# B laid out in DRAM and SBUF with four states side by side per time step, and its product with x walked in that layout by GpSimd

## The chip, the cores and the metric

One core of a Trainium2 chip runs the whole program. The metric is the device time of one execution in microseconds (us). The engines of the core run their own queues of instructions in order and wait for each other through semaphores: PE (TensorE, matmuls; PEld is its loading of weights), DVE (VectorE), ACT (ScalarE), POOL (GpSimd), and SP (SyncE), which issues the DMAs here.

## What is computed

The input x has 32 sequences (batches) of 512 steps with 256 channels. Three layers follow each other, each added to its own input: a feed-forward layer with blockwise 4-bit quantization (counted half), a selective state-space layer, and the first layer once more. The change lies in the state-space layer, whose input is normalized first:

```python
BC = x @ W_in + b_in
Bm, Cm = (BC[..., :N], BC[..., N:])            # N = 16 states
dt = jax.nn.softplus((x @ W_dt1 + b_dt1) @ W_dt2 + b_dt2)
dt = jnp.clip(dt, 1e-07, 1000000.0)
tmp = A * dt[..., None]
A_bar = jnp.exp(tmp)
B_barX = jnp.expm1(tmp) / tmp * dt[..., None] * Bm[:, :, None, :] * x[..., None]
...
_, h = jax.lax.associative_scan(combine, (A_bar, B_barX), axis=1)   # h[t] = A_bar[t] h[t-1] + B_barX[t]
return jnp.sum(h * Cm[:, :, None, :], axis=-1) + D * x
```

So for each channel and each of 16 states there is one recurrence over 512 steps. Bm and Cm depend on the step and the state, not on the channel.

## The kernel before

All data are 32-bit floats apart from the quantizer's bf16 helpers. The loop runs over the 32 batches. For each batch there are an input load, `ffn` (first layer), `ssm` (the state-space layer), `ffn` again and an output store; several batches are in flight at once.

In `ssm`, channels lie on the 128 partitions, in NC = 2 halves (index c), and the 512 steps lie along the free dimension. L is 512, N is 16, NG = 2 states make a group and XG = 4 states make a bigger one. Per batch:

- `project` (PE) and `project bias` (ACT, L1658) make `bc`, a tile of 96 partitions: 64 rows that lead to dt, 16 rows of B and 16 of C, one state per partition, 512 steps each.
- `rows` (SP, L1661) stores the 32 rows of B and C in DRAM, one row of 2 KB per state. This is done since B and C are needed on all 128 partitions.
- `load b` (SP, L1697) reads four states at a time back, the same 8 KB for all 128 partitions, into `bn`; `load c` (SP, L1707) reads two states at a time, 4 KB for each partition, into `cn`. Two buffers exist of each.
- `x b` (POOL, L1701) multiplies `bn` with x, in two halves of 256 steps, into `bx`. x does not depend on the state, so it is repeated over the four states. `bn` and `bx` hold state after state, 512 steps (2 KB) each, but the instruction goes through them step by step with the four states innermost. Each instruction has 256 x 4 = 1024 elements per partition. Two buffers of `bx` exist.
- For each state, `exp` (ACT, L1714) and `tanh` (ACT, L1717) make A_bar and a half-way value of expm1, and three DVE instructions of 512 elements follow: `e` (L1722) finishes expm1 in PSUM (tile `eb`), `e x b` (L1725) multiplies it with 1/A and with this state's `bx`, and `scan` (L1728) runs the recurrence into `hs`. `e x b` reads `eb` from PSUM and `bx` from SBUF and writes `eb`.
- `h c` (POOL, L1731) multiplies two states of `hs` with `cn`, 1024 elements per partition without gaps; `sum states` (PE, L1737) adds the states up in PSUM.

POOL also does part of the feed-forward layer: `product` (L1611) and the quantizer's `value` (L1482; tiles x_q and h_q), where a block's scale is repeated over its 16 elements. DVE makes the quantizer's `quotient` (L1457), the tops of the blocks (L1451) and the statistics of the norms (L1414, L1416).

The order of the work is written out. Every operation is given to a planner (class `Plan`) with a name, and tables (`WHEN` for the batches in the middle, four others for the first two and last two) hold a due time for each name and count; `PERIOD` = 3379 is added per batch. `Plan.run` puts out operations by due time among those whose inputs have been put out, so the tables set the order on each engine's queue, SP's among them. Nothing is reordered after that: an instruction that waits holds up all that stand behind it on its engine. On SP, each batch's `rows` is followed by loads of the old batch's C and by the new batch's first loads.

Of the kernel before, what the change touches and what calls it, by code (L numbers as in the profile page):

```python
# [31 lines left out]
    "in load": (307,),  # L32
    "ffn 0 stats": (1353, 1162, 433, 1372),
    "ffn 0 mean": (1534, 1207, 2280, 3568),
    "ffn 0 var + eps": (-3072,),
    "ffn 0 rstd": (3743,),
    "ffn 0 - mean": (4137,),
    "ffn 0 shift": (4475,),
    "ffn 0 normal": (4908, 2828, 6516, 4907),
    "ffn 0 x top": (6592,),  # L40
    "ffn 0 x scale": (6720,),
    "ffn 0 x rinv": (6812,),
    "ffn 0 x quotient": (6837,),
    "ffn 0 x square": (6261,),
    "ffn 0 x curve": (6856,),
    "ffn 0 x grid": (4711,),
    "ffn 0 x rounded": (6976,),
    "ffn 0 x value": (6142,),
    "ffn 0 xqT turn": (4710, 4914),
    "ffn 0 xqT turned": (7146, 7155),  # L50
    "ffn 0 tile 0 gate": (7210, 7319),
    "ffn 0 tile 0 silu": (7161, 2717),
    "ffn 0 tile 0 up": (7401, 7534),
    "ffn 0 tile 0 up copy": (7351, 6546),
    "ffn 0 tile 0 product": (7515,),
    "ffn 0 tile 0 h top": (5636,),
    "ffn 0 tile 0 h scale": (7181,),
    "ffn 0 tile 0 h rinv": (7180,),
    "ffn 0 tile 0 h quotient": (7627,),
    "ffn 0 tile 0 h square": (7711,),  # L60
    "ffn 0 tile 0 h curve": (7562,),
    "ffn 0 tile 0 h grid": (7878,),
    "ffn 0 tile 0 h rounded": (7861,),
    "ffn 0 tile 0 h value": (7221,),
    "ffn 0 tile 0 turn h": (8266, 8252),
    "ffn 0 tile 0 turned h": (8274, 7803),
    "ffn 0 tile 0 down": (8290,),
    "ffn 0 tile 0 sum": (8486,),
    "ffn 0 tile 1 gate": (7304, 7296),
    "ffn 0 tile 1 silu": (2718, 7291),  # L70
    "ffn 0 tile 1 up": (7647, 7600),
    "ffn 0 tile 1 up copy": (7666, 7543),
    "ffn 0 tile 1 product": (7866,),
    "ffn 0 tile 1 h top": (5728,),
    "ffn 0 tile 1 h scale": (7954,),
    "ffn 0 tile 1 h rinv": (7992,),
    "ffn 0 tile 1 h quotient": (8122,),
    "ffn 0 tile 1 h square": (6213,),
    "ffn 0 tile 1 h curve": (8129,),
    "ffn 0 tile 1 h grid": (8248,),  # L80
    "ffn 0 tile 1 h rounded": (7560,),
    "ffn 0 tile 1 h value": (8160,),
    "ffn 0 tile 1 turn h": (8336, 8293),
    "ffn 0 tile 1 turned h": (8522, 8488),
    "ffn 0 tile 1 down": (8042,),
    "ffn 0 tile 1 sum": (8701,),
    "ffn 0 tile 2 gate": (8119, 7928),
    "ffn 0 tile 2 silu": (2794, 7879),
    "ffn 0 tile 2 up": (8264, 8273),
    "ffn 0 tile 2 up copy": (7802, 8296),  # L90
    "ffn 0 tile 2 product": (6444,),
    "ffn 0 tile 2 h top": (8264,),
    "ffn 0 tile 2 h scale": (8601,),
    "ffn 0 tile 2 h rinv": (8613,),
    "ffn 0 tile 2 h quotient": (8695,),
    "ffn 0 tile 2 h square": (8710,),
    "ffn 0 tile 2 h curve": (8735,),
    "ffn 0 tile 2 h grid": (6475,),
    "ffn 0 tile 2 h rounded": (8841,),
    "ffn 0 tile 2 h value": (8721,),  # L100
    "ffn 0 tile 2 turn h": (9122, 9107),
    "ffn 0 tile 2 turned h": (8382, 5692),
    "ffn 0 tile 2 down": (9225,),
    "ffn 0 tile 2 sum": (9325,),
    "ffn 0 tile 3 gate": (7716, 8127),
    "ffn 0 tile 3 silu": (7942, 2826),
    "ffn 0 tile 3 up": (9143, 8936),
    "ffn 0 tile 3 up copy": (9141, 8666),
    "ffn 0 tile 3 product": (6825,),
    "ffn 0 tile 3 h top": (7046,),  # L110
    "ffn 0 tile 3 h scale": (9360,),
    "ffn 0 tile 3 h rinv": (9385,),
    "ffn 0 tile 3 h quotient": (9493,),
    "ffn 0 tile 3 h square": (9353,),
    "ffn 0 tile 3 h curve": (9316,),
    "ffn 0 tile 3 h grid": (9623,),
    "ffn 0 tile 3 h rounded": (8097,),
    "ffn 0 tile 3 h value": (7051,),
    "ffn 0 tile 3 turn h": (9844, 9871),
    "ffn 0 tile 3 turned h": (8951, 8950),  # L120
    "ffn 0 tile 3 down": (9947,),
    "ffn 0 tile 3 sum": (9935,),
    "ssm stats": (7942, 8890, 7943, 10031),
    "ssm mean": (8545, 9204, 9821, 10049),
    "ssm var + eps": (10005,),
    "ssm rstd": (10126,),
    "ssm - mean": (10045,),
    "ssm shift": (10041,),
    "ssm normal": (8232, 9649, 10217, 6497),
    "ssm xT turn": (9246, 9640),  # L130
    "ssm xT turned": (10313, 10313),
    "ssm project": (8090,),
    "ssm project bias": (10457,),
    "ssm rows": (9313,),
    "ssm dt2": (8051, 8384),
    "ssm softplus": (10541, 10544),
    "ssm dt": (10508, 9631),
    "ssm skip": (11627, 13151),
    "ssm load b": (10786, 11246, 11120, 11686, 11954, 12465, 12823, 13159),
    "ssm x b": (10531, 9490, 10597, 11073, 11565, 11669, 12052, 11677, 12468, 7925, 12412, 12743,  # L140
        10352, 13417, 13583, 13798),
    "ssm load c": (11311, 10847, 11325, 11777, 11406, 11777, 11792, 11811, 11862, 11989, 12014,
        13532, 12026, 13786, 13913, 14209),
    "ssm exp": (10700, 10946, 11034, 11044, 11258, 11259, 11240, 11087, 11664, 11907, 11912,
        11913, 11913, 11913, 12345, 12225, 12490, 12516, 12519, 12719, 13029, 12929, 13085,
        13066, 13322, 13323, 13131, 13275, 13770, 13502, 13450, 13777),
    "ssm tanh": (10731, 10973, 11042, 11241, 11279, 11258, 11650, 11646, 11864, 11909, 11914,
        12018, 12214, 12091, 12507, 12248, 12577, 12707, 12733, 12708, 13057, 13025, 13268,
        13199, 13328, 13306, 13456, 13766, 13916, 13780, 13979, 13991),
    "ssm e": (10235, 9833, 11092, 10967, 11584, 11594, 11721, 11628, 11858, 10249, 12181, 12182,  # L150
        12313, 12247, 11634, 12407, 10023, 11182, 12898, 12892, 12567, 12674, 13226, 13200,
        13587, 13542, 13704, 13137, 13847, 13907, 13549, 13615),
    "ssm e x b": (10234, 11095, 11134, 11301, 11610, 11613, 11820, 11799, 11874, 11985, 12189,
        12197, 12293, 12291, 12523, 12433, 12657, 12747, 12939, 12915, 13073, 13160, 13343,
        13246, 13653, 13627, 13677, 13828, 13932, 13921, 13697, 13549),
    "ssm scan": (10562, 11165, 11199, 11372, 11621, 11627, 11861, 11859, 11823, 12056, 12207,
        12220, 12406, 12322, 12686, 11614, 12691, 12839, 12882, 12278, 13164, 13197, 13427,
        13340, 13701, 13678, 13732, 13863, 13947, 13946, 13889, 13614),
    "ssm h c": (10223, 11578, 11018, 12017, 10603, 7293, 12497, 12580, 12784, 11899, 9665, 13688,
        13687, 13052, 12718, 14391),  # L160
    "ssm sum states": (11141, 11893, 11713, 6003, 12437, 12481, 12951, 12996, 12840, 13502,
        13309, 12629, 11669, 13999, 14218, 14616),
    "ssm residual": (12495, 14304),
    "ssm y": (12977, 12964),
    "ffn 1 stats": (11977, 14749, 12432, 14433),
    "ffn 1 mean": (13948, 14834, 14136, 14679),
    "ffn 1 var + eps": (13592,),
    "ffn 1 rstd": (14752,),
    "ffn 1 - mean": (13902,),
    "ffn 1 shift": (14930,),  # L170
    "ffn 1 normal": (14540, 14539, 14508, 14424),
    "ffn 1 x top": (15016,),
    "ffn 1 x scale": (15039,),
    "ffn 1 x rinv": (15062,),
    "ffn 1 x quotient": (15152,),
    "ffn 1 x square": (13043,),
    "ffn 1 x curve": (15194,),
    "ffn 1 x grid": (15023,),
    "ffn 1 x rounded": (15270,),
    "ffn 1 x value": (15381,),  # L180
    "ffn 1 xqT turn": (11956, 15071),
    "ffn 1 xqT turned": (15299, 15398),
    "ffn 1 tile 0 gate": (13330, 12186),
    "ffn 1 tile 0 silu": (15594, 15471),
    "ffn 1 tile 0 up": (13636, 13273),
    "ffn 1 tile 0 up copy": (15646, 15624),
    "ffn 1 tile 0 product": (15453,),
    "ffn 1 tile 0 h top": (15815,),
    "ffn 1 tile 0 h scale": (15851,),
    "ffn 1 tile 0 h rinv": (15898,),  # L190
    "ffn 1 tile 0 h quotient": (15929,),
    "ffn 1 tile 0 h square": (16045,),
    "ffn 1 tile 0 h curve": (16044,),
    "ffn 1 tile 0 h grid": (16085,),
    "ffn 1 tile 0 h rounded": (13362,),
    "ffn 1 tile 0 h value": (15806,),
    "ffn 1 tile 0 turn h": (16345, 16437),
# [1608 lines left out]
```

## Time and profile before

| what | value |
|---|---|
| two timed runs | 3768.75 and 3769.3 us, median 3769.03 |
| the profiled execution's own time | 3767.57 us |
| its span, first to last instruction | 3765.8 us |
| granted TensorE clock over the span | 0.976 |
| packets of the SP queue's DMAs | 147952, 574.87 MB, 44.8% of 16 engines |
| longest waits of DVE | `e` for ACT's `tanh` 146.8 us; the tops of the blocks for `product` 69.1; `e x b` for `x b` 42.0 |
| waits of POOL for `bn` | 8.3 us in 18 times, longest 1.5 |
| duration of `x b`, shortest, median, longest | 2553, 2578, 2671 ns |
| duration of `e x b`, the same | 658, 753, 762 ns |
| `rows`, issue to landing, the same | 1.6, 1.6, 3.3 us |

A row of a group reads: line, engine, operation, output<-inputs by the program's names, their shapes, count, then busy time, mean duration in ns, then the engine's idle time just before these instructions and who ended it. "SPq" is an instruction that issues a DMA. In a list of stretches, the columns are the stretch, its length, busy time and count for each engine, granted clock, DMA share and GB/s. Shares of "16 engines" are those of the core's 16 DMA engines.

### The profile page before, as it was taken

The page shows a single profiled execution, that of the slowest core. Times are in us where ns is not written, and L with a number is a line of the kernel's source. Part 1 is how long each engine was busy: PE and PEld are TensorE (multiplying, and loading weights), DVE is VectorE, ACT ScalarE, POOL GpSimd, SP SyncE. Part 2 cuts the span into 40 slices and gives each one's busy share as a digit, 9 for nine tenths or more (in the row PEclk, how much of TensorE's full clock was granted, in tenths as well). Part 3 has the DMA queues.
Part 4 walks back from the last instruction along what each step waited for, and adds up shares of the span by engine and source line. Part 5 has one row for each costly group of instructions (what it writes and reads, how often), then busy time and mean ns, then how long its engine had stood idle before and what let it go on. Part 6 is the DMA issues. An engine that isn't in the chain of part 4 may idle for free.

```text
span 3765.8 us, 50230 instructions
## 1 busy us (share of the span) xinstructions
PE 3336.0 (89%) x16501; PEld 2445.0 (65%) x16698; DVE 3387.0 (90%) x5152; ACT 3423.8 (91%) x5848; POOL 3562.6 (95%) x2059
## 2 busy tenths in 40 slices
PE   6688999998988998999998989998999998999967
PEld 4456666666666666666666666666666666666745
DVE  4799999999999999999999999999999999999984
ACT  5789999999999999999999999999999999999974
POOL 3799999999999999999999999999999999999994
PEclk9899999999999999999999999999999999999989
DMA  1344454444454444454444454444444454444451
GB/s 47 143 162 157 158 172 144 170 155 158 152 177 148 169 152 160 152 178 149 168 151 161 155 175 151 164 155 160 159 167 157 157 163 155 163 155 162 152 174 34
DMA packets 149783, 578.29 MB, mean 154 GB/s; under 512 B 15568, under 2 KB 49936, under 8 KB 116752
## 3 DMA queue, kind: packets, MB, share of 16 engines
q1 hardware_dynamic: 147952, 574.87, 44.8%
q8 instruction: 132, 2.16, 0.2%
q14 instruction: 131, 1.07, 0.1%
q10 hardware_dynamic: 1568, 0.18, 0.0%
HBM read 556.12 MB, written 18.87 MB: 153 GB/s over the span
## 4 chain that ended last, share of the span: by engine, by line
POOL 38%; PE 23%; DVE 17%; ACT 12%; issue 9%; DMA 0%; POOLq 0%; SPq 0%; DVEq 0%; ACTq 0%
POOL hs L1731 14%; PE pt L1588 12%; POOL bx L1701 11%; DVE hs L1728 5%; POOL h_q L1482 5%; DVE eb L1725 4%; POOL h L1611 3%; PE py L1737 3%; POOL x_q L1482 3%; PE pt L1634 3%; DVE eb L1722 2%; ACT ab L1714 2%; DVE q L1457 2%; ACT eb L1717 2%; PE pt L1622 2%
## 5 line engine op out<-in xcount | busy, mean ns | idle before, releaser
L1588 PE MATMUL pt<-w_guT,xqT 128*128 128x352 f32 x4096 | 1339.4, 471 | 12.6 <-ACT sl L1598 6.5
L1701 POOL TENSOR_TENSOR bx<-xT,bn 128x1024 f32<-128x1024 f32 x512 | 1318.5, 2582 | 10.5 <-DMA bn<-rows 8.3
L1731 POOL TENSOR_TENSOR hs<-hs,cn 128x1024 f32<-128x1024 f32 x512 | 1208.5, 2366 | 8.6 <-PE pt L1588 2.3
L1728 DVE TENSOR_TENSOR_SCAN hs<-ab,eb 128x512 f32<-128x512 f32 x1024 | 1203.8, 1202 | 12.4 <-POOL dt L1673 2.9
L1588 PEld LDWEIGHTS pt<-w_guT,xqT 128*128 128x128 f32 x4096 | 760.6, 195 | 391.6 <-ACT sl L1598 29.4
L1722 DVE SCALAR_TENSOR_TENSOR eb<-ab,eb 128x512 f32<-128x512 f32 x1024 | 692.6, 685 | 152.3 <-ACT eb L1717 146.8
L1725 DVE SCALAR_TENSOR_TENSOR eb<-eb,a_inv,bx 128x512 f32<-128x512 f32 x1024 | 745.1, 747 | 49.9 <-POOL bx L1701 42.0
L1717 ACT ACTIVATE eb<-dt,a_half 128x512 f32<-128x512 f32 x1024 | 706.3, 697 | 34.3 <-DVE hs L1728 33.8
L1634 PE MATMUL pt<-w_dT,hqT 128*128 128x256 f32 x3072 | 720.6, 384 | 13.1 <-ACT hqT L1627 13.0
L1714 ACT ACTIVATE ab<-dt,a_sb 128x512 f32<-128x512 f32 x1024 | 720.8, 727 | 2.0 <-DVE hs L1728 0.5
L1634 PEld LDWEIGHTS pt<-w_dT,hqT 128*128 128x128 f32 x3072 | 571.4, 191 | 125.0 <-ACT hqT L1627 37.0
L1737 PE MATMUL py<-ident,hs 128*128 128x128 f32 x4096 | 544.7, 282 | 74.7 <-POOL hs L1731 74.6
L1737 PEld LDWEIGHTS py<-ident,hs 128*128 128x128 f32 x4096 | 485.8, 146 | 163.0 <-POOL hs L1731 95.0
L1611 POOL TENSOR_TENSOR h<-h,sl 128x704 f32<-128x704 f32 x256 | 432.1, 1688 | 51.2 <-ACT h L1608 43.1
L1482 POOL TENSOR_TENSOR h_q<-h_q,h_sc 128x704 f32<-128x704 f32 x258 | 359.6, 1394 | 34.1 <-ACT h_q L1481 31.8
L1622 PE MATMUL pt<-ident,h_q 128*128 128x128 f32 x1536 | 242.0, 280 | 135.5 <-POOL h_q L1482 69.7
L1622 PEld LDWEIGHTS pt<-ident,h_q 128*128 128x128 f32 x1536 | 170.7, 142 | 238.9 <-POOL h_q L1482 117.9
L1451 DVE TENSOR_REDUCE q<-h 128x44 f32<-128x704 f32 x258 | 228.0, 884 | 103.0 <-POOL h L1611 69.1
L1598 ACT ACTIVATE sl<-pt 128x352 f32<-128x352 f32 x512 | 223.7, 462 | 66.6 <-PE pt L1588 62.8
L1627 ACT COPY hqT<-pt 128x256 f32<-128x256 f32 (+1 forms) x512 | 238.5, 480 | 45.4 <-PE pt L1622 45.0
L1470 PEld LDWEIGHTS <-eye 128*128 128x128 bf16 x1300 | 124.2, 98 | 219.3 <-issue 132.4
L1470 PE MATMUL q<-h_m,eye 128*128 128x192 bf16 (+1 forms) x871 | 190.5, 304 | 68.9 <-ACT h_m L1463 59.2
(74 smaller groups left out, 4020.8 us busy)
## 6 DMA issues: line engine op xcount, KB each, us to landing
bn<-rows SPq DMA_DIRECT2D x256, 1024.0 KB, 6.6
cn<-rows SPq DMA_DIRECT2D x512, 512.0 KB, 4.3
x<-in_L_attn_x_dram SPq DMA_DIRECT2D x32, 512.0 KB, 5.3
out_dram<-x SPq DMA_DIRECT2D x32, 512.0 KB, 5.2
rows<-bc SPq DMA_DIRECT2D x32, 64.0 KB, 1.6
xn<-in_L_ffn_w_up_dram SPq DMA_DIRECT2D x6, 128.0 KB, 2.3
h<-in_L_ffn_w_down_dram SPq DMA_DIRECT2D x2, 352.0 KB, 3.3
xn<-in_L_ffn_w_gate_dram SPq DMA_DIRECT2D x5, 128.0 KB, 2.2
```

What stands on the lines that cost most here:

```text
L1482: op("POOL", f"{tag} value", lambda: g.tensor_tensor(blocks(dst()), blocks(dst()), spread(scale()), ALU.mult), [dst, scale], [dst])
L1588: pe.matmul(to()[:, :HALF], lhsT=xqT()[:, c, j * P : (j + 1) * P], rhs=w_guT()[:, c, o : o + HALF], start=(c == 0), stop=(c == NC - 1),)
L1611: op("POOL", "product", lambda sl=sl, h=h: g.tensor_tensor(h(), h(), sl(), ALU.mult), [h, sl], [h])
L1634: pe.matmul(po()[:, :DM], lhsT=hqT()[:, k, :], rhs=w_dT()[:, k, :], start=(k == 0), stop=False,)
L1701: op("POOL", "x b", lambda c=c, bx=bx, bn=bn, t=t: g.tensor_tensor(bx()[:, :, t].rearrange("p n l -> p l n"), xT()[:, c, t].unsqueeze(2).t ...
L1714: op("ACT", "exp", lambda c=c, i=i, k=k, ab=ab: s.activation(ab()[:, i, :], dt()[:, c, :], AF.Exp, scale=a_sb[:, c, k : k + 1]), [(dt, c)] ...
L1717: op("ACT", "tanh", lambda c=c, i=i, k=k, eb=eb: s.activation(eb[i](), dt()[:, c, :], AF.Tanh, scale=a_half[:, c, k : k + 1]), [(dt, c)], ...
L1722: op("DVE", "e", lambda i=i, ab=ab, eb=eb: v.scalar_tensor_tensor(eb[i](), ab()[:, i, :], 1.0, eb[i](), ALU.add, ALU.mult), [(ab, i), eb[i ...
L1725: op("DVE", "e x b", lambda c=c, i=i, k=n + i, eb=eb, bx=bx: v.scalar_tensor_tensor(eb[i](), eb[i](), a_inv[:, c, k : k + 1], bx()[:, k % ...
L1728: op("DVE", "scan", lambda i=i, h=h, ab=ab, eb=eb: v.tensor_tensor_scan(h()[:, i, :], ab()[:, i, :], eb[i](), 0.0, ALU.mult, ALU.add), [(a ...
L1731: op("POOL", "h c", lambda h=h, cn=cn: g.tensor_tensor(flat(h()), flat(h()), flat(cn()), ALU.mult), [h, cn], [h])
L1737: pe.matmul(py()[:, j, :], lhsT=h()[:, i, j * P : (j + 1) * P], rhs=ident, is_transpose=True, start=False, stop=False, skip_group_check=True,)
```

## The change

B is laid out with four states side by side per step. In DRAM, `rows` is split in two: `rows_b` holds [4 groups, 512 steps, 4 states] and `rows_c` holds C as before. B is stored by four DMAs per batch; each takes four partitions of `bc` with 512 steps and writes single elements with a step of 16 bytes. `bn` and `bx` become [128, 512 steps, 4 states]. `load b` still reads 8 KB without gaps for each partition. `x b` goes through `bn` and `bx` in the order in which they lie. `e x b` reads one state of `bx`, so 512 elements with a step of 16 bytes. Nothing else in the arithmetic, the buffers or their number changes.

```diff
-        rows = new(dr, [2 * N, L], F32, "rows", 2)
-        op("SP", "rows", lambda: nc.sync.dma_start(rows(), bc()[R:, :]), [bc], [rows])
+        rows_b = new(dr, [N // XG, L, XG], F32, "rows_b", 2)
+        rows_c = new(dr, [N, L], F32, "rows_c", 2)
+
+        def interleave():
+            with nc.allow_non_contiguous_dma(reason="B of one step side by side, 32 KB per batch"):
+                for i in range(N // XG):
+                    nc.sync.dma_start(
+                        rows_b()[i].rearrange("l n -> n l"),
+                        bc()[R + i * XG : R + (i + 1) * XG, :])
+
+        op("SP", "rows b", interleave, [bc], [rows_b])
+        op("SP", "rows c", lambda: nc.sync.dma_start(rows_c(), bc()[R + N :, :]), [bc], [rows_c])
...
-                    bn, bx = (new(st, [P, XG, L], F32, tag, 2) for tag in ("bn", "bx"))
+                    bn, bx = (new(st, [P, L, XG], F32, tag, 2) for tag in ("bn", "bx"))
                     op("SP", "load b", lambda n=n, bn=bn: nc.sync.dma_start(
-                        bn(), rows()[n : n + XG, :].partition_broadcast(P)), [rows], [bn])
+                        bn(), rows_b()[n // XG].partition_broadcast(P)), [rows_b], [bn])
                     for o in range(0, L, L * NG // XG):
                         t = slice(o, o + L * NG // XG)
                         op("POOL", "x b", lambda c=c, bx=bx, bn=bn, t=t: g.tensor_tensor(
-                            bx()[:, :, t].rearrange("p n l -> p l n"),
+                            bx()[:, t, :],
                             xT()[:, c, t].unsqueeze(2).to_broadcast([P, L * NG // XG, XG]),
-                            bn()[:, :, t].rearrange("p n l -> p l n"), ALU.mult),
-                           [(xT, c), bn], [(bx, o)])
+                            bn()[:, t, :], ALU.mult), [(xT, c), bn], [(bx, o)])
                 cn = new(st, [P, NG, L], F32, "cn", 2)
                 op("SP", "load c", lambda n=n, cn=cn: nc.sync.dma_start(
-                    cn(), rows()[N + n : N + n + NG, :].partition_broadcast(P)), [rows], [cn])
+                    cn(), rows_c()[n : n + NG, :].partition_broadcast(P)), [rows_c], [cn])
...
-                        eb[i](), eb[i](), a_inv[:, c, k : k + 1], bx()[:, k % XG, :],
+                        eb[i](), eb[i](), a_inv[:, c, k : k + 1], bx()[:, :, k % XG],
                         ALU.mult, ALU.mult), [eb[i], bx], [eb[i]])
```

The tables' due times are new throughout, with the same PERIOD, so the order differs on every engine. On SP, `rows b` and `rows c` stand where `rows` stood. The program has the same number of instructions of each kind on PE, DVE, ACT (its 287 loads of function tables among them) and POOL, apart from instructions that only wait; SP issues 1007 DMAs for 879.

## The prediction

> **What bounds the kernel now.** I read the page's first part first: who is busy, and of which span.
>
> ```profile
> span 3765.8 us, 50230 instructions
> PE 3336.0 (89%) x16501; PEld 2445.0 (65%) x16698; DVE 3387.0 (90%) x5152; ACT 3423.8 (91%) x5848; POOL 3562.6 (95%) x2059
> ```
>
> POOL (GpSimd) is busiest, but four engines lie within 6 points, so a gain on one is soon stopped by the next. Shares over the span mix start and end with the middle, so I cut one batch out of the middle: `rows` is issued at 1333.0 and again at 1446, so the period is 113 us. The columns are stretch, length, then busy time (count) of PE, PEld, DVE, ACT, POOL, then clock, DMA share and GB/s.
>
> ```profile
> 1333.00:1446.00 113.00, 102.79 (x516) 75.80 (x521) 105.11 (x161) 106.12 (x183) 111.11 (x65) 0.98 0.49 159
> ```
>
> POOL idles 1.9 us of 113 and sets the pace; ACT idles 6.9, DVE 7.9, PE 10.2. Then the groups of instructions, the edited two and those that can price them:
>
> ```profile
> L1701 POOL TENSOR_TENSOR bx<-xT,bn 128x1024 f32<-128x1024 f32 x512 | 1318.5, 2582 | 10.5 <-DMA bn<-rows 8.3 <-DVE hs L1728 0.8 <-POOL h L1611 0.5
> L1731 POOL TENSOR_TENSOR hs<-hs,cn 128x1024 f32<-128x1024 f32 x512 | 1208.5, 2366 | 8.6 <-PE pt L1588 2.3 <-DVE hs L1728 1.9 <-PE pt L1622 1.1
> L1482 POOL TENSOR_TENSOR x_q<-x_q,x_sc 128x1024 f32<-128x1024 f32 x67 | 129.9, 1939 | 40.5 <-ACT x_q L1481 28.6 <-DVE pt L1455 11.8
> ...
> L1725 DVE SCALAR_TENSOR_TENSOR eb<-eb,a_inv,bx 128x512 f32<-128x512 f32 x1024 | 745.1, 747 | 49.9 <-POOL bx L1701 42.0 <-DVE mv L1416 0.4
> L1457 DVE SCALAR_TENSOR_TENSOR q<-h,q 128x704 f32<-128x704 f32 x258 | 227.8, 883 | 1.6
> L1457 DVE SCALAR_TENSOR_TENSOR q<-xn,pt 128x1024 f32<-128x1024 f32 x67 | 81.7, 1220 | 3.6 <-ACT x_q L1481 3.2
> ```
>
> `x b` (L1701, 2582 ns) walks four states in turn, 2 KB apart; `h c` (L1731) has the same 1024 elements without gaps and two full inputs; `x value` (L1482, x_q) also has no gaps, and its second input repeats, as x does in `x b`. Last, how much time lies between bc, out of which B goes to DRAM, and the first use of B. The timelines of SP, ACT, POOL and DVE in that batch:
>
> ```profile
> 1332.28 0.69 ACT L1658 ACTIVATE bc<-pt,b_p_sb 96x512 f32<-96x512 f32 x1
> ...
> 1332.99 0.32 SPq L1661 DMA_DIRECT2D rows<-bc  x1
> 1333.41 0.36 SPq L1707 DMA_DIRECT2D cn<-rows  x1
> 1334.63 0.32 SPq L1697 DMA_DIRECT2D bn<-rows  x1
> ...
> 1344.52 5.11 POOL L1701 TENSOR_TENSOR bx<-xT,bn 128x1024 f32<-128x1024 f32 x2
> ...
> 1349.65 0.76 DVE L1725 SCALAR_TENSOR_TENSOR eb<-eb,a_inv,bx 128x512 f32<-128x512 f32 x1 [1.44 <-POOL bx L1701]
> ```
>
> The page's DMA issues give a median of 6.6 us from issue to landing for bn and 1.6 for `rows`. So bn lands at 1341.2 and POOL takes it up at 1344.5: 3.3 us to spare.
>
> **POOL: x b without gaps.** 512 instructions of 2582 ns. Ends: 2366 (`h c`: no gaps, two full inputs) and 1939 (`x value`: no gaps, one input repeated). The new `x b` is the second form with blocks of 4 for 16, so I take 1939: 0.64 us less, 10.3 us per batch, 329 us in all, to POOL's share alone. (The Trainium skill, "GPSIMD Engine Reference", Performance pitfalls, has reads with a byte step over 8 cost about 2.9 cycles an element against 1.9, the same direction as 2582 against 1939.) POOL then needs 101 of the 113 us; next in line are ACT at 106 and DVE at 105, so this part alone is worth about 32 x 3.4 = 110 us, not 329.
>
> **DVE: e x b now reads bx with a step of 16 bytes.** 1024 instructions of 747 ns. No row shows a DVE read with a step. Low end 0: the same elements in the same operation; a gain is excluded, since nothing is left out. Middle: POOL's price for gaps, (2582 - 1939)/1024 = 0.63 ns an element, gives 0.32 us. High end: one more element time per element; L1457 grows from 883 to 1220 ns over 320 elements, 1.05 ns each, so 512 x 1.05 = 0.54 us. I take the high end: DVE streams one element per 1.05 ns, and I suppose that a fetch that comes late costs it a whole element time. 1024 x 0.54 = 552 us, 17.3 per batch: DVE goes from 105.1 to 122.4 and becomes the bound. Of its idle time (7.9 per batch, mostly waits for ACT and POOL, which now run ahead) I strike half, 32 x 3.9 = 125 us.
>
> Against the rule: "SBUF — State Buffer" in the Trainium skill, the note on cachelines under Door 1, has 16-byte lines that need two hits each for full rate; this read hits each line once. It states no price; by it the 0 end is out and the sum stays as I made it, while POOL's 0.63 would give 222 us less. It is the rule that speaks most against this change.
>
> **SP: B goes to DRAM element by element.** The one `rows` DMA (32 x 2 KB) becomes four for B with a step of 16 bytes in DRAM, 8192 packets of 4 bytes per batch, and one for C. The trace has 4-byte loads at its start, on the ACT queue (q10): packets, MB and share of 16 engines, in the DMA queues of 5.4 to 6.0 us, when nothing else ran, and of 6.36 to 6.46:
>
> ```profile
> DMA packets 237, 0.00 MB, mean 2 GB/s; under 512 B 237, under 2 KB 237, under 8 KB 237
> ...
> q10 hardware_dynamic: 237, 0.00, 19.1%
> ```
>
> ```profile
> q10 hardware_dynamic: 129, 0.00, 70.4%
> q1 hardware_dynamic: 9, 0.01, 25.9%
> ```
>
> In the second stretch the engines are full (96%) and a packet takes 0.704 x 16 x 100 ns / 129 = 8.7 ns of an engine. In the first they are 19% busy: packets come at 237 in 0.6 us, one per 2.5 ns, so something feeds them no faster. Ends for the 8192: all 16 engines at 8.7 ns, 4.5 us; four engines (each of the DMAs reads four partitions) at the first stretch's pace per engine, 0.6 x 16/237 = 40 ns, 82 us. Four engines at 8.7 ns give 17.9 us; the feed's pace, whatever the number of engines, 20.7. I take 20.7.
>
> "DMA: Bandwidth & Descriptors" in the skill (Why a DMA increments its semaphore by 16) lets the slowest dimension set the number of engines, here four: by it 4.5 us is excluded and at least 17.9 remains; no DMA so narrow is in this trace.
>
> What waits: SP issues in order, `load b` waits for the first of the four, the old batch's `load c` stands behind it, and the packets of both stand behind the other three in the same queue. From 1332.99, plus 20.7, plus bn's own 6.6 - 1.6 = 5.0 us of transfer, bn lands at 1358.7 for 1341.2: 17.5 later. POOL had 3.3 to spare, and its two `x b` are 1.3 shorter: bx comes 12.9 late. DVE itself comes there 2.2 later (four slowed `e x b` lie between). So each batch adds a wait of 10.7 us at `e x b`, for POOL first and DVE behind it; 32 x 10.7 = 342 us. At 4.5 us it is nothing (3.3 covers it), at 82 it is 72 us. The four issues (0.5 us each in the ACT queue at the start) run beside this.
>
> **Order.** All due times are new; instruction counts and the 287 table loads on ACT are the same. I take 0, since an instruction that stands elsewhere on an engine that is not the bound only changes where that engine waits; where it lands on DVE's path the cover is gone, and for that I keep 38 us (1%) either way.
>
> **Sum.** Against the profiled execution's 3767.6 us (1.5 under the median of 3769.0): + 552 - 125 + 342 = 4537, say 4540; POOL's 329 are gained where nothing waits for them.
>
> **Rivals.**
> - *DVE alone* (0.12): the 8192 packets hide. 3768 + 552 - 125 = 4195. For it: 16 engines at 8.7 ns; against: the feed's pace.
> - *DMA alone* (0.18): the step is free on DVE. Without the 2.2, the wait is 12.9: 3768 - 125 + 32 x 12.9 = 4056. For it: L1725's other operands lie in PSUM, and DVE has one SBUF stream only.
> - *Packets at 15 to 40 ns* (0.20): at 40, 3768 + 552 - 125 + 32 x 72 = 6500; at 28 ns D is 57, the wait 47, the time 5700. For it: writes of 4 bytes to DRAM are nowhere in the trace.
> - *Faster* (0.10): POOL's shorter `x b` shortens the period, since POOL sets it now, until ACT stops it: 106.1 plus twice POOL's present idle, 109.6; 3768 - 32 x 3.4 = 3660. For it: POOL's 95%; against: DVE is only 6 us behind. It decides while `e x b` grows by less than (113 - 105.1 - 3.5)/32 = 0.14 us and the packets stay under about 5 us.
> - That the change doesn't do what it says (x b not faster) changes nothing here: POOL at 111 stays under DVE.
>
> **Numbers.** My forecast, both prices, has 0.40 and its own range 4300 to 4850. The range 3900 to 5700 leaves out the faster case and the upper half of the slow packets, 0.2. Its low end is *DMA alone* at 17.9 us (3966) less 1% and some. Chances, with 2% as what a measurement of this kernel can tell: faster 0.08, same 0.04 (edges of the faster and the DMA case), slower 0.88.
>
> **What would show it.** `x b` near 1940 ns; `e x b` near 1290; DVE at the top of the busy list; a row rows_b<-bc with 20 us from first issue to last landing; POOL waiting for bn some 14 us once per batch. Wrong if `e x b` stays at 750, or if no wait for bn appears.

## The result, and the profile after

The changed kernel takes 5394.51 us (two runs, 5392.84 and 5396.18) for 3769.03: a ratio of 1.431, 95% interval 1.425 to 1.437. It is slower, as forecast, but by 1625 us where the forecast had 771 (4540).

The first lines of the page of the kernel after: the span, and the busy time, share and count of each engine.

```profile
span 5394.4 us, 50649 instructions
PE 3478.0 (64%) x16698; PEld 2525.4 (47%) x16698; DVE 3768.1 (70%) x5152; ACT 3456.7 (64%) x5848; POOL 3302.9 (61%) x2059
```

DVE does lead the list, with 381 us more than before, but it is busy for 70% of the span only. No engine is the bound any more: the kernel waits. The three groups that answer to those of before, in the kernel after:

```profile
L1738 DVE SCALAR_TENSOR_TENSOR eb<-eb,a_inv,bx 128x512 f32<-128x512 f32 x1024 | 1165.1, 1160 | 1476.0 <-POOL bx L1715 1468.9
L1715 POOL TENSOR_TENSOR bx<-xT,bn 128x1024 f32<-128x1024 f32 x512 | 1032.3, 2023 | 1497.8 <-DMA bn<-rows_b 1438.7
L1744 POOL TENSOR_TENSOR hs<-hs,cn 128x1024 f32<-128x1024 f32 x512 | 1213.3, 2370 | 289.4 <-DVE hs L1741 121.9
```

`x b` went from 2582 to 2023 ns, and `e x b` from 747 to 1160. What weighs more stands behind the second bar: 1469 us of idle time of DVE ahead of `e x b`, put down to `x b`, and 1439 us of POOL ahead of `x b`, put down to the load of bn. The list of waits of the kernel after (total, times, longest) says how it is spread:

```profile
DVE eb L1738 <- POOL bx L1715: 1468.9, 32, 55.9
POOL bx L1715 <- DMA bn<-rows_b: 1438.7, 39, 57.8
```

32 waits for 32 batches: 45.9 us each. The timelines of SP, POOL and DVE around one of them (start, length, engine, line, count; the idle time ahead in brackets):

```profile
2056.27 40.70 SPq L1670 DMA_DIRECT2D rows_b<-bc  x4
2097.02 13.09 SPq L1675 DMA_DIRECT2D rows_c<-bc  x1
2110.21 0.36 SPq L1711 DMA_DIRECT2D bn<-rows_b  x1
...
2118.61 3.97 POOL L1715 TENSOR_TENSOR bx<-xT,bn 128x1024 f32<-128x1024 f32 x2 [50.91 <-DMA bn<-rows_b]
...
2122.61 1.13 DVE L1738 SCALAR_TENSOR_TENSOR eb<-eb,a_inv,bx 128x512 f32<-128x512 f32 x1 [48.88 <-POOL bx L1715]
```

Before, SP issued `rows` in 0.32 us and the next load 0.1 us later. Now it hangs at four element stores and at `rows c` behind them for 53.9 us, and issues nothing else. `load b` goes out at 2110.21, and POOL can begin 8.4 us later. How fast the elements go is seen in the kernel after's DMA queues of 2097 to 2110, when nothing else moves (packets, MB, share of 16 engines):

```profile
DMA packets 2047, 0.01 MB, mean 1 GB/s; under 512 B 2047, under 2 KB 2047, under 8 KB 2047
q1 hardware_dynamic: 2047, 0.01, 27.5%
```

One packet of 4 bytes per 13000/2047 = 6.35 ns. 8192 of them at 6.35 ns are 52 us per batch. The share (4.4 engines' worth) is no count of the engines at work: in two runs below it is 2.0 engines' worth and 168.5% of all 16.

Two stretches of the kernel after, a batch and the end of the wait, in the columns of before:

```profile
2000.00:2165.00 165.00, 106.73 (x514) 78.39 (x512) 115.39 (x159) 106.52 (x182) 101.86 (x64) 0.82 0.42 107
2097.00:2111.00 14.00, 0.00 (x0) 0.00 (x0) 0.00 (x0) 0.00 (x0) 0.00 (x0) 0.50 0.27 3
```

A batch takes about 165 us for 113. In the second stretch not one of the five engines has an instruction under way.

### The profile page after: what moved, and what is told of

It is laid out like the page before. It is cut to its first block, busy times and chain, and to the rows that moved or that the text cites. A ratio compares the mean times of both kernels' runs of the same rounds, so it can differ in the third digit from the quotient of the medians.

```text
span 5394.4 us, 50649 instructions
## 1 busy us (share of the span) xinstructions
PE 3478.0 (64%) x16698; PEld 2525.4 (47%) x16698; DVE 3768.1 (70%) x5152; ACT 3456.7 (64%) x5848; POOL 3302.9 (61%) x2059
## 4 chain that ended last, share of the span: by engine, by line
DVE 52%; issue 33%; POOL 5%; SPq 4%; PE 3%; ACT 2%; DMA 1%; POOLq 0%; DVEq 0%; ACTq 0%
DVE hs L1741 17%; DVE eb L1738 14%; DVE eb L1735 8%; DVE q L1461 4%; SPq L1670 3%; DVE q L1455 3%; POOL bx L1715 2%; DVE stats L1418 2%; POOL hs L1744 2%; DVE q L1459 1%; PE pt L1638 1%; DVE pt L1455 1%; PE pt L1592 1%; DVE mv L1420 1%; DVE pt L1459 1%
## 5 line engine op out<-in xcount | busy, mean ns | idle before, releaser
L1738 DVE SCALAR_TENSOR_TENSOR eb<-eb,a_inv,bx 128x512 f32<-128x512 f32 x1024 | 1165.1, 1160 | 1476.0 <-POOL bx L1715 1468.9
L1715 POOL TENSOR_TENSOR bx<-xT,bn 128x1024 f32<-128x1024 f32 x512 | 1032.3, 2023 | 1497.8 <-DMA bn<-rows_b 1438.7
L1592 PE MATMUL pt<-w_guT,xqT 128*128 128x352 f32 x4096 | 1364.2, 474 | 103.8 <-ACT hqT L1631 48.3
L1626 PE MATMUL pt<-ident,h_q 128*128 128x128 f32 x1536 | 266.0, 297 | 1340.7 <-POOL h_q L1486 1235.3
L1626 PEld LDWEIGHTS pt<-ident,h_q 128*128 128x128 f32 x1536 | 189.4, 150 | 1439.2 <-POOL h_q L1486 1269.6
L1638 PE MATMUL pt<-w_dT,hqT 128*128 128x256 f32 x3072 | 739.9, 392 | 54.7 <-ACT hqT L1631 54.5
L1735 DVE SCALAR_TENSOR_TENSOR eb<-ab,eb 128x512 f32<-128x512 f32 x1024 | 690.6, 687 | 21.5 <-ACT ab L1727 18.5
L1638 PEld LDWEIGHTS pt<-w_dT,hqT 128*128 128x128 f32 x3072 | 589.1, 196 | 176.3 <-ACT hqT L1631 74.9
L1750 PEld LDWEIGHTS py<-ident,hs 128*128 128x128 f32 x4096 | 505.8, 151 | 179.7 <-POOL hs L1744 129.7
L1474 PE MATMUL q<-h_m,eye 128*128 128x512 bf16 (+1 forms) x1032 | 215.2, 334 | 193.3 <-ACT h_m L1467 192.7
L1612 ACT COPY h<-pt 128x352 f32<-128x352 f32 x512 | 219.0, 446 | 63.7 <-PE pt L1592 63.1
```

The costliest lines, as they stand in the source:

```text
L1592: pe.matmul(to()[:, :HALF], lhsT=xqT()[:, c, j * P : (j + 1) * P], rhs=w_guT()[:, c, o : o + HALF], start=(c == 0), stop=(c == NC - 1),)
L1626: pe.transpose(pt()[:, i * P : (i + 1) * P], hq()[:, kcol[k] : kcol[k] + P], ident)
L1638: pe.matmul(po()[:, :DM], lhsT=hqT()[:, k, :], rhs=w_dT()[:, k, :], start=(k == 0), stop=False,)
L1715: op("POOL", "x b", lambda c=c, bx=bx, bn=bn, t=t: g.tensor_tensor(bx()[:, t, :], xT()[:, c, t].unsqueeze(2).to_broadcast([P, L * NG // XG ...
L1735: op("DVE", "e", lambda i=i, ab=ab, eb=eb: v.scalar_tensor_tensor(eb[i](), ab()[:, i, :], 1.0, eb[i](), ALU.add, ALU.mult), [(ab, i), eb[i ...
L1738: op("DVE", "e x b", lambda c=c, i=i, k=n + i, eb=eb, bx=bx: v.scalar_tensor_tensor(eb[i](), eb[i](), a_inv[:, c, k : k + 1], bx()[:, :, k ...
```

## The experiments

The theory after the result: (1) the step of 16 bytes makes DVE the bound, at a price of its own; (2) the element stores take over 50 us per batch and hold SP's queue, so everything behind them is late. Rivals: what costs is that `x b` waits for this particular data; or that the layout, or the new order of the work, costs by itself. Each run stands beside the kernel before on the same chip (3759 to 3765 us); they are single runs unless an interval is given. The kernel before took 3769 us where the changed kernel was timed, so a difference between a run here and 5394.51 is uncertain by some 10 us.

**Element stores alone.** The kernel before, with the stores added; nobody reads them.

```diff
+        unread = new(dr, [N // XG, L, XG], F32, "unread", 2)
...
             nc.sync.dma_start(rows(), bc()[R:, :])
+                for i in range(N // XG):
+                    nc.sync.dma_start(
+                        unread()[i].rearrange("l n -> n l"),
+                        bc()[R + i * XG : R + (i + 1) * XG, :])
```

> The kernel before, with the four DMAs of single elements added behind its `rows` store, into a DRAM tile that nobody reads. Theory: the DMAs hold the SP queue for about 53 us per batch, so every later load is late by that, whoever needs the data: POOL's wait for bn of about 50 us per batch, 3768 + 32 x 50 = 5370 us. Rival: the cost is the wait for B's own data; with the data unread the time stays at 3770 to 3800.

Measured: 5419.65 for 3761.40, so +1658. The timeline of SP in this kernel:

```profile
2068.22 41.00 SPq L1667 DMA_DIRECT2D unread<-bc  x4
2109.26 13.66 SPq L1717 DMA_DIRECT2D cn<-rows  x1
2123.03 0.37 SPq L1707 DMA_DIRECT2D bn<-rows  x1
```

And its waits:

```profile
DVE eb L1735 <- POOL bx L1711: 1701.6, 34, 58.2
POOL hs L1741 <- DMA cn<-rows: 1477.5, 29, 55.0
```

The stores, which feed nothing, cost as much as the whole change. POOL now waits for `load c` of the old batch: that load has nothing to do with the stores and only stands behind them on SP. So the held queue alone is enough for the whole loss, and lateness of B's own data is not needed for it. In the change both come together, since `load b` stands behind the stores and needs their elements too; its trace does not separate the two.

**The change without element stores.** The changed kernel; B goes to DRAM in 16 rows of 2 KB, so its values lie in the wrong order.

```diff
-                for i in range(N // XG):
-                    nc.sync.dma_start(
-                        rows_b()[i].rearrange("l n -> n l"),
-                        bc()[R + i * XG : R + (i + 1) * XG, :])
+            nc.sync.dma_start(
+                rows_b().rearrange("g l s -> g (l s)").rearrange("g (s l) -> (g s) l", l=L),
+                bc()[R : R + N, :])
```

> The changed kernel with B stored in one DMA of 16 rows of 2 KB (so B reaches the product in the wrong order); loads, x b and e x b as changed. Theory: the waits for bn are the element stores alone; DVE with e x b at 1160 ns needs 105.1 + 32 x 0.413 = 118.3 us per batch and keeps half its idle time, 122, so 3768 + 32 x 9 = 4060 us. Rival: the new order itself causes waits for bn or cn, then 4300 or more.

Measured: 3933.57, +172, and 126 less than expected. Its engines, and `e x b`, on its page:

```profile
PE 3406.3 (87%) x16698; PEld 2470.4 (63%) x16698; DVE 3770.5 (96%) x5152; ACT 3455.0 (88%) x5848; POOL 3303.2 (84%) x2059
...
L1736 DVE SCALAR_TENSOR_TENSOR eb<-eb,a_inv,bx 128x512 f32<-128x512 f32 x1024 | 1167.8, 1162 | 10.5 <-POOL bx L1713 0.3
```

DVE is the bound at 96%, and `e x b` waits for nothing. Layout and new order cost 172 us, and the stores the other 1461 (5394.51 - 3933.57), 45.7 us per batch, against the wait of 45.9 seen above. (Measured against its own kernel before, the change costs 1625, which leaves 1453.) The 172 us hold layout and order together; no run has the new order alone.

**The step alone.** The kernel before; `e x b` reads its 512 elements of `bx` with a step of 16 bytes, in another run with one of 8 bytes; the values are thereby mixed up.

```diff
-                        eb[i](), eb[i](), a_inv[:, c, k : k + 1], bx()[:, k % XG, :],
+                        eb[i](), eb[i](), a_inv[:, c, k : k + 1],
+                        flat(bx()).rearrange("p (l s) -> p l s", s=XG)[:, :, k % XG],
```

> The kernel before, with e x b alone reading bx with a step of 16 bytes (so states and steps are mixed up); everything else as before. Theory: the step alone makes e x b 1160 ns, DVE needs 118.3 us per batch and becomes the bound, 122 with half its idle time: 4060 us. Rival: the 1160 ns came from POOL working in the same tile in the new way; then e x b stays near 750 and the time near 3770.

> The same with a step of 8 bytes. By a rule of lines of 16 bytes that want two hits each, 8 bytes are free: 750 ns and 3770 us. Rival: any step costs in proportion to the bytes passed over: between 750 and 1160, some 890 ns, DVE at 109.6 per batch, 3830 us.

Measured: 3938.36 with 16 bytes and 3770.08 with 8, for 3764.03. The group in the run with 16 bytes:

```profile
L1725 DVE SCALAR_TENSOR_TENSOR eb<-eb,a_inv,bx 128x512 f32<-128x512 f32 x1024 | 1169.5, 1163 | 13.3 <-POOL bx L1701 2.3
```

And in the run with 8:

```profile
L1725 DVE SCALAR_TENSOR_TENSOR eb<-eb,a_inv,bx 128x512 f32<-128x512 f32 x1024 | 744.5, 746 | 51.1 <-POOL bx L1701 43.2
```

The step of 16 bytes costs 416 ns (0.81 ns an element), that of 8 nothing. The run with 16 comes out where the change without element stores does (3934), although there `x b` is 560 ns shorter: so once DVE is the bound, POOL's gain buys nothing, unless the new order costs just what it saves.

**Half the stores.** The changed kernel, with two of the four groups of B stored in rows, in the wrong order.

```diff
+                    if i < 2:
+                        nc.sync.dma_start(rows_b()[i].rearrange("l n -> n l"), half)
+                    else:
+                        nc.sync.dma_start(
+                            rows_b()[i].rearrange("l s -> (l s)").rearrange("(s l) -> s l", l=L), half)
```

> The changed kernel with two of the four stores of B by single elements and two in rows (their part of B in the wrong order). Theory: the hold of the SP queue goes with the packets, 27 us for 53, and the wait with it: 5394 - 32 x 26.5 = 4550 us. Rival: the hold has a fixed part per batch; then clearly more than 4550.

Measured: 4557.48. That is the 4550 expected. From none to half it grows by 624 us, from half to all by 837. The second half costs 26.2 us per batch, the full time of 4096 elements at 6.35 ns (26.0); the first costs 19.5, as if some 6.5 us of it were hidden by the slack that the prediction counts.

**More engines, by way of DRAM.** The changed kernel; all 32 rows go to DRAM first, and four DMAs rearrange B from DRAM to DRAM, with 512 steps as the outer dimension in one run, with the four states in the other.

```diff
-                        rows_b()[i].rearrange("l n -> n l"),
-                        bc()[R + i * XG : R + (i + 1) * XG, :])
+                        rows_b()[i],
+                        rows_c()[i * XG : (i + 1) * XG, :].rearrange("n l -> l n"))
```

> The changed kernel, with B stored as before in rows of 2 KB and then laid out by four DMAs from DRAM to DRAM with the steps outermost, still 8192 packets of 4 bytes. Theory: a packet takes some 26 ns of its engine, and steps outermost let all 16 engines share: 512 x 26 = 13 us instead of 53, a wait of some 10 us per batch over the run without element stores: about 4400 us. Rival: descriptors are made at one per 6.5 ns whatever the engines: 53 us again, 5400 us or more.

> The same as the run with the steps outermost, but with the four states outermost, so four engines. Theory: 53 us per batch as in the changed kernel, 5450 us. Rival: four-byte stores out of SBUF are what is slow; then it takes no longer than the run with the steps outermost.

Measured: 5311.34 and 5617.25. The theory had 4400 for the first and missed by 900. SP in that run:

```profile
2026.11 18.52 SPq L1670 DMA_DIRECT2D rows_b<-rows_c  x4
2044.73 13.54 SPq L1711 DMA_DIRECT2D bn<-rows_b  x1
```

SP's four stores take less (18.5 us), but the elements still take long to land, and bn, which needs them, waits: POOL got to `x b` at 2080.21, 54 us after the first issue. The second run missed its 5450 by 167: there the stores hold SP for 45 us again and `load b` behind them for 14 more. It is 306 us slower than the first, so its rival, that the two take the same, falls. How many engines took part was not counted in either; the outer dimension is worth 306 us, which is not the main thing, and the price of an element had to be looked for elsewhere.

**What makes an element dear.** The kernel before, with four more DMAs of 2048 pieces per batch behind `rows`, whose data nobody uses. Only the DMAs differ; this is the first of them, and the table has the others.

```diff
             nc.sync.dma_start(rows(), bc()[R:, :])
+                for i in range(4):
+                    nc.sync.dma_start(
+                        unread()[:, :, i], bc()[:R, i * 32 : (i + 1) * 32])
```

> The kernel before, with four DMAs behind rows that load 8192 single elements per batch from DRAM into a tile in SBUF that nobody reads; each runs over 64 partitions. The stores of single elements held the queue for 41 us (5 ns per piece) and brought the kernel before to 5420. If it is the number of pieces that costs, whatever they are and however many partitions they run over (the feed): 41 us again, 5200 to 5450. If the price is one of small writes into DRAM: 512 pieces per engine at the 8.7 ns of the loads at the start are 4.5 us, the feed's 2.5 ns each are 20.5; with some 3 us to spare that is 3810 to 4330. If it is a price per piece on each engine (26 ns with four engines): 13 us, 4080.

> The kernel before, with four DMAs behind rows that store 8192 single elements per batch with a step of 16 bytes into an unread DRAM tile, out of 64 partitions each instead of four. Number of pieces: 5200 to 5450 as with four partitions. Per engine (26 ns each on four engines, now spread over 16): 13 us, 4080. Small writes into DRAM, whatever the engine: like the first, 5200 to 5450.

> As the run with the 16-byte step out of 64 partitions, but every element goes 256 bytes apart, and the four DMAs into regions of their own. If neighbours in one line of DRAM make the small writes wait for each other: much faster than that run (below 4400 where that one is above 5200). If it is the number of pieces or the write as such: the same within 2%.

> As the run with 256 bytes between elements, but pieces of 64 bytes, 128 bytes apart: the same 8192 pieces per batch with 16 times the data (0.5 MB). If the number of pieces costs: the same within 3%. If a write below 64 bytes is what costs: below 4400.

> The kernel before, with 8192 single elements stored into unread DRAM 256 bytes apart, out of four partitions per DMA. Out of 64 partitions the same came to 4057 (256 bytes apart) and 4782 (16 bytes); out of four with 16 bytes to 5420. If only the nearness in DRAM counts: about 4057. If only the price per engine counts (the 13 us of the 64 partitions now on four engines for 16): above 5300. Both: 4400 to 5000.

> The kernel before, with 8192 single elements stored out of 64 partitions 16 bytes apart, each of the four DMAs into a region of its own (the run with the step of 16 bytes let all four fill the same region, 4782). If the four DMAs hinder each other in the same bytes: near 4057, the time of the step of 256 bytes. If neighbours within one DMA are enough: 4700 to 4850.

> The kernel before, with 8192 single elements stored out of 64 partitions, each DMA into its own region, 64 bytes apart. The same came to 4735 with 16 bytes and to 4057 with 256. If elements hinder each other within 64 bytes alone: 4020 to 4100. If it is distance as such, or a wider piece of DRAM: 4200 to 4700.

> As the run with 64 bytes, but 32 bytes apart: two elements in 64 bytes for one, and for four with 16. If elements hinder each other within 64 bytes: 4200 to 4600, between 4057 and 4735. If within 32: as with 64 bytes, 4020 to 4100.

| 8192 pieces per batch | partitions per DMA | step in DRAM | time, us | more than before |
|---|---|---|---|---|
| 4-byte stores (as in the change) | 4 | 16 B | 5419.65 | 1658 |
| the same | 4 | 256 B | 4554.59 | 794 |
| the same, four DMAs in one region | 64 | 16 B | 4781.90 | 1017 |
| the same, each DMA in its own region | 64 | 16 B | 4734.97 | 974 |
| the same | 64 | 32 B | 4424.31 | 665 |
| the same | 64 | 64 B | 4144.61 | 386 |
| the same | 64 | 256 B | 4056.99 | 292 |
| 64-byte stores | 64 | 128 B | 3823.55 | 59 |
| 4-byte loads, into 64 partitions | 64 | 8 B (read) | 3910.09 | 145 |

It is not the number of pieces: as many loads cost 145 us, and as many stores of 64 bytes cost 59. It is the store of 4 bytes close to the one before. With steps of 16, 32 and 64 bytes it costs 974, 665 and 386; going on to 256 bytes saves only another 94. The run with 64 bytes fell between its two expectations, 45 us over the one and 55 under the other: most of the price is gone at 64 bytes, and not all of it. Whether 64 bytes is an edge or the price falls with distance was not measured. The first run out of 64 partitions (4782) also lay between its expectations, since two things count: it is dearer out of four partitions than out of 64, at 16 bytes (1658 for 1017) as at 256 (794 for 292). At 16 bytes that comparison changes two things, since out of four partitions the four also write into the same 16 bytes.

The pace, from stretches in which hardly anything but these packets moves. 64 partitions, 16 bytes, each DMA in its own region, 2090 to 2100, just after the first issue:

```profile
DMA packets 5296, 0.02 MB, mean 2 GB/s; under 512 B 5296, under 2 KB 5296, under 8 KB 5296
```

64 partitions, 16 bytes, one region, 2126 to 2136, late in the batch:

```profile
DMA packets 2190, 0.03 MB, mean 3 GB/s; under 512 B 2189, under 2 KB 2189, under 8 KB 2189
q1 hardware_dynamic: 2189, 0.01, 168.5%
```

Four partitions, 256 bytes, 2146 to 2166:

```profile
DMA packets 5791, 0.04 MB, mean 2 GB/s; under 512 B 5790, under 2 KB 5790, under 8 KB 5790
q1 hardware_dynamic: 5790, 0.02, 12.7%
```

64 partitions, 256 bytes, 2159 to 2164:

```profile
DMA packets 5267, 0.09 MB, mean 17 GB/s; under 512 B 5235, under 2 KB 5235, under 8 KB 5267
```

That is one per 1.9, 4.57, 3.45 and 0.95 ns; the change has 6.35. Out of 64 partitions at 16 bytes the pace falls off within a batch, and over most of one (7933 packets from 2114 to 2137) it is 2.9 ns. Far apart, four partitions for 64 make it 3.6 times slower; near each other 2.2 times over a batch, and 1.4 times in its late part. What limits 64 partitions there is not shown.

**Do the engines hinder each other?** The changed kernel, where each DMA takes one state of every group, so that its four partitions write 8 KB apart and not into the same 16 bytes.

```diff
-                        rows_b()[i].rearrange("l n -> n l"),
-                        bc()[R + i * XG : R + (i + 1) * XG, :])
+                        rows_b()[:, :, i],
+                        bc()[R + i : R + N : XG, :])
```

> The changed kernel, with each of the four DMAs taking one state of each group (four partitions that write 8 KB apart) for four states of one group (four partitions that write into the same 16 bytes). Same elements, same places, same number. If what is slow is that several engines write into the same few bytes at the same time: well below the changed kernel, under 4900. If neighbours within one engine's own run are enough, or if it is four engines for the work of sixteen: 5300 to 5500 again.

Measured: 5201.47, which is 193 us less than the change: under the 5300 of the one expectation, but far above the 4900 that would have made this the cause. Stores near each other within one partition's own run are enough to make them slow, as the run with own regions shows too (974 us for 292 at 256 bytes).

**POOL's gain without the layout.** The kernel before, where `x b` takes two states and all 512 steps at once, state after state, and x is repeated as a whole. Nothing moves in DRAM or SBUF, and `x b` has no gaps all the same.

```diff
-                    for o in range(0, L, L * NG // XG):
-                        t = slice(o, o + L * NG // XG)
...
-                            bx()[:, :, t].rearrange("p n l -> p l n"),
-                            xT()[:, c, t].unsqueeze(2).to_broadcast([P, L * NG // XG, XG]),
-                            bn()[:, :, t].rearrange("p n l -> p l n"), ALU.mult),
+                    for o in range(0, XG, NG):
...
+                            bx()[:, o : o + NG, :],
+                            xT()[:, c, :].unsqueeze(1).to_broadcast([P, NG, L]),
+                            bn()[:, o : o + NG, :], ALU.mult),
```

> The kernel before with x b alone changed: it goes through bn and bx as they lie, two states of 512 steps in each instruction, x repeated once per state. Layout, stores and e x b stay. Theory: it becomes the form of h c, 2366 ns for 2582, POOL needs 107.7 us per batch for 111.1, and ACT at 106.1 is next: 3768 - 32 x 3 = 3670 us. Rival: POOL's gain is swallowed by waits on ACT and DVE in this order: 3740 to 3770.

Measured: 3650.76 (four runs, 3646.73 to 3656.49), a ratio of 0.970 to the kernel before, 95% interval 0.968 to 0.972: faster than both kernels. `x b` on its page, and its stretch of 2000 to 2500:

```profile
L1700 POOL TENSOR_TENSOR bx<-xT,bn 128x1024 f32<-128x1024 f32 x512 | 1208.4, 2367 | 13.1 <-DMA bn<-rows 11.3
```

```profile
2000.00:2500.00 500.00, 464.86 (x2363) 342.36 (x2389) 480.76 (x730) 484.76 (x831) 493.81 (x293) 1.00 0.48 165
```

POOL gains 215 ns for each `x b` (2582 to 2367), 512 x 0.215 = 110 us, and the kernel 113: POOL still sets the pace (494 of 500 us), so each microsecond counts in full.

## Why the prediction was wrong

- **POOL: x b.** Predicted 1939 ns, measured 2023. The form with blocks of 4 lies a little above the row with blocks of 16. That this would be worth nothing once another engine waits held.
- **DVE: e x b.** Predicted + 0.54 us, measured + 0.413, between the ends 0.32 and 0.54: 423 us for 552. Of the idle time I struck half, 125 us; by the run without element stores 218 went (3766 - 3387 = 379 us before, 3932 - 3771 = 161 there). DVE's whole busy time, in which instructions that overlap count once, grew by 384 and not by 423. So the net term was 172 us and not 427. The mechanism was right, a late element costing 0.81 ns and not the whole 1.05 that I supposed; all sizes leaned the same way, and the sum was 255 us too high here.
- **The rule on lines.** The Trainium skill's page "SBUF — State Buffer" (the note on cachelines under Door 1) wants two hits on each 16-byte line for full rate. The two runs agree: at a step of 8 bytes each line is hit twice and the 746 ns are those of the read without gaps; at 16 it is hit once and 1163.
- **SP: B element by element. This is the step that failed.** I took D = 20.7 us, from the pace of 2.5 ns per packet of 4-byte *loads* at the start of the trace; the stores came at 6.35 ns, and the queue was held for 53.9 us. I had called the 2.5 ns a feed that goes no faster; my own second stretch, 129 packets in 100 ns, already had 0.78, and the run of loads had 4442 packets from 2084 to 2089, 1.1 ns. It was no limit, and the 8.7 ns of an engine rested on a share that is no count of engines. The rest of the chain was right as a sum: my working lets the wait be 10.0 us less than D, which for 53.9 gives 43.9, and 45.9 were measured. The term became 1461 us for 342. Where a store differs from a load, I had no row; I knew that (the rival said so) and still took the loads' value, though I had an upper end of 82 us. With 256 bytes between the elements, stores out of four partitions gave 3.45 ns, a hold of 29.4 us (SP from 2144.70 to 2174.10) and 794 us: dearer than my 20.7 us even there. The other 24.5 us of the 53.9 come with the nearness of the elements in DRAM, which I did not weigh at all.
- **"The four issues (0.5 us each) run beside this."** Wrong too: the median issue took 11.8 us. I read this as a queue that is full; the traces show only that SP stands still. In the change this may be no extra cost, as `load b` needs the elements anyhow; but it also made the old batch's `load c` late, and with unread stores it cost 1658 us all by itself.
- **The rule on engines.** The skill's "DMA: Bandwidth & Descriptors" (Why a DMA increments its semaphore by 16) gives four engines for four partitions. Between four and 64 partitions that would be a factor of 4, an estimate from this rule; far apart 3.6 was measured, near each other 2.2. The same page (Specifications) has transfers under 512 bytes pay for a read-modify-write. By that alone, stores of 64 bytes and stores of 4 bytes far apart should be as dear; they cost 59 and 292 us for 974, so here size and nearness decide.
- **The order.** I took 0. The run without element stores has the new order and lies 5 us from the run with the old order and the step alone. That agrees, as far as POOL's shorter `x b` is worth nothing there; the two could also cancel.
- **The rivals.** "Packets at 15 to 40 ns" is what happened in its size: its 28 ns on four engines are 57 us per batch, and SP was held for 53.9. Its 5700 less the 255 us of the DVE term is 5445, for 5394 measured. Its reason, that no row had a store of 4 bytes, was right; the nearness was not in it. The range held the time through this rival; the forecast did not.

The sum, as it should have been: 3768 + 172 + 1461 = 5401, for 5394.5. It closes by construction, since both terms are differences of runs. With the 1469 us of waiting from the trace in place of the 1461 it is 5409.

What stays open: what inside the chip makes near stores slow, the DMA engines or the memory behind them. That four partitions write into the same bytes at once is 193 of it, that successive DMAs fill one region 43 (1017 to 974), and neither is the main part.

## What to carry to other kernels

A layout that makes one instruction smooth has to be paid where it is made and where else it is read; price those two first, and each by a row of its own kind: a store is not a load, and elements that land next to each other are not elements far apart. A slow DMA costs more than its own data when loads stand behind it in the queue. If the same instruction can be made smooth by the order in which it walks the data as they lie, as here, nothing has to be paid, though it gains less (2367 ns, where the new layout gave 2023).

## What the runs showed that I had not expected

- Stores of 4 bytes cost by their neighbours: 6.35 ns each at a step of 16 bytes out of four partitions, 0.95 at 256 bytes out of 64; as many loads of 4 bytes into 64 partitions cost 145 us.
- An issue is not short behind such stores: 11.8 us in the median for the element stores, and 12.4 for the `rows c` behind them, which is itself 16 rows of 2 KB.
- A step of 8 bytes in one input of `e x b` is free (746 ns for 747); one of 16 costs 0.81 ns an element.
- While all engines waited, the granted clock stood at 0.50 (0.82 over the batch shown, 0.98 before). It cost little: a matmul of the costliest group (`pt<-w_guT,xqT`) took 474 ns in the mean for 471 before, and one of the group that waits longest (`pt<-ident,h_q`) 297 for 280.
